# A two-layer graph attention kernel: the order of TensorE's work written out by hand

## The chip, the cores and the metric

The kernel runs on one core of one Trainium2 chip. A core has five engines that run side by side: TensorE (PE, matmuls and transposes; PEld is its weight load), VectorE (DVE), ScalarE (ACT), GpSimd (POOL) and SyncE (SP), which here issues all transfers. Each engine takes its instructions in the order in which the program gives them, and waits at an instruction until what it needs is there. The time is the device time of one execution, in microseconds (us); the figure is the median of three runs.

## The reference, cut to what matters

There are 32 graphs of 512 nodes with 512 features, an adjacency matrix each, and weights that all graphs share. Each graph goes through a normalisation, two attention layers (four heads of 256 features, then one of 512) and a residual sum. All of it is in f32; only the masks are in bf16.

```python
h = relu(layernorm(x))                       # [32, 512, 512]
mask = (adj > 0) | eye(512)
def gat_layer(x, mask, W, a_src, a_dst, bias, concat):
    xl = (x @ W).reshape(B, N, H, F)
    asrc, adst = einsum(xl, a_src), einsum(xl, a_dst)          # [B, N, H]
    e = leaky_relu(asrc[:, :, None] + adst[:, None], 0.2)
    attn = softmax(where(mask, e, -1e9), axis=1)               # over source nodes
    out = einsum('bsdh,bshf->bdhf', attn, xl)
    ...
h = elu(gat_layer(h, mask, W1, att_src1, att_dst1, b1, concat=True))     # 4 heads x 256
out = x + gat_layer(h, mask, W2, att_src2, att_dst2, b2, concat=False)   # 1 head x 512
```

## The kernel before

**Stages of a graph.** A graph's 512 nodes are four tiles of 128 rows. `front` normalises x (VectorE; a power on GpSimd), transposes it on TensorE (`pht`, 16 transposes of 128x128) into `ht`, makes the mask `m` from adj and its transpose `mt` (`pm`, 16 transposes in bf16). `project1`, the first product, makes `xl` in eight accumulator tiles (`pxl`, 16 matmuls each, two heads a tile; two more columns a head hold the scores of the attention vectors, which `weights` folded into W1). `soft` is the softmax of a layer: the scores are transposed to a row (`pas`), stored to DRAM and loaded back spread over all partitions; VectorE takes the masked maximum over each of the 128-row tiles (`junk`, L205: 16 in layer 1, 4 in layer 2); the shifts made from the maxima are transposed (`prr`) and sent the same way; then ScalarE takes two exponentials for each tile of `p` (L227, L230) and VectorE takes their maximum and applies the mask (L234, L235). `gather1` is the first aggregation: for each head two accumulator tiles (`po`, L288, 32 matmuls a head), scaled by the inverse sum into `z`; `turn` transposes `z` (`pz`), and an exponential and two VectorE operations make `h1`, two turns a head. `project2`, the second product, makes `xl2` from `h1` in four tiles of 32 matmuls (`pxm`), each emptied by ScalarE (L315). `gather2` is the second aggregation (`po`, L333, four tiles of 16) and adds x and b2 (`xr`), loaded again and added by GpSimd.

**Order.** The loop of `tile_gat` goes over i. One pass holds the first product of graph i+1, the second aggregation of i-1, the second product of i and the first aggregation of i+1. The other generators (`front` of i+2, the softmaxes) are on a list `side`, and `run` takes one or more of their steps after each step of the main one. This is the order of the program's text; a planner then orders the instructions of each engine by this priority and by its own estimates of when each will be ready. It decides where in TensorE's queue a `prr` or `pas` stands.

**Buffers.** PSUM has eight banks: two accumulator tiles of two banks (tag `mm`), three banks for transposes (`tp`), one for the row turns `pas` and `prr` (`sc`). `xl`, `xl2` and `h1` are there once, `p` four times, the spread rows `orr` twice, `adj` twice, `xr` three times.

Of the kernel before, what the change touches and what calls it, by code (L numbers as in the profile page):

```python
# [28 lines left out]
def tile_gat(  # L29
# [60 lines left out]
    def weights():  # L90
# [30 lines left out]
    def load(b):  # L121
        XT[b], ADJ[b] = [], []
        for t in range(NT):
            xt = work.tile([P, D], F32, tag="x", name=f"x{b}_{t}", bufs=4)
            nc.sync.dma_start(xt, x[b, t * P : (t + 1) * P, :])
            XT[b].append(xt)
            a = work.tile([P, N], I32, tag="adj", name=f"adj{b}_{t}", bufs=2)
# [3 lines left out]
    def front(b):  # L131
# [11 lines left out]
        for t in range(NT):  # L143
# [4 lines left out]
            ps = psum.tile([P, KT, P], F32, tag="tp", name=f"pht{b}_{t}", bufs=3)  # L148
# [4 lines left out]
        del XT[b]  # L153
        m = work.tile([P, NT, N], BF16, tag="m", name=f"m{b}", bufs=3)
# [7 lines left out]
        for d in range(NT):  # L162
            ps = psum.tile([P, N], BF16, tag="tp", name=f"pm{b}_{d}", bufs=3)
# [5 lines left out]
            yield  # L169

    def soft(b, layer, n, cols, give):
# [8 lines left out]
        def spread(v, rows, per, tag, bufs):  # L180
# [4 lines left out]
            sb = work.tile([k, P], F32, tag=f"r{tag}", name=f"r{tag}{name}")  # L185
            nc.vector.tensor_copy(sb, ps)
            dr = dram.tile([k, P], F32, tag=f"d{tag}", name=f"d{tag}{name}")
            nc.sync.dma_start(dr, sb)
            got = []
            for i in range(0, rows, per):  # L190
                o = work.tile([P, per, N], F32, tag=f"o{tag}", name=f"o{tag}{name}_{i}", bufs=bufs)
# [6 lines left out]

        asr = spread(sc[:, 0].rearrange("p h t -> p (h t)"), n, n, "as", 1)[0]
        yield  # L200
        mx = work.tile([P, n, NT], F32, tag=f"mx{layer}", name=f"mx{name}")
        for h in range(n):
            for d in range(NT):
                junk = work.tile([P, N], BF16, tag="junk", name=f"junk{name}_{h}_{d}", bufs=1)
                nc.vector.tensor_tensor_reduce(  # L205
                    out=junk, in0=asr[:, h, :], in1=MASKT[b][:, d, :], scale=1.0, scalar=-BIG,
                    op0=OP.add, op1=OP.max, accum_out=mx[:, h, d : d + 1],
                )
                if d % 2:
                    yield  # L210
        if layer == 2:
            del MASKT[b]
        ad = sc[:, 1]
        top = work.tile([P, n, NT], F32, tag=f"top{layer}", name=f"top{name}")
        nc.vector.tensor_add(top, mx, ad)
        nc.vector.scalar_tensor_tensor(top, top, SLOPE, top, op0=OP.mult, op1=OP.max)
        r = work.tile([P, n, 2, NT], F32, tag=f"r{layer}", name=f"r{name}")
        nc.vector.tensor_sub(r[:, :, 0, :], ad, top)
        nc.vector.scalar_tensor_tensor(r[:, :, 1, :], ad, SLOPE, top, op0=OP.mult, op1=OP.subtract)
        rr = spread(r.rearrange("p h i t -> p (h i t)"), 2 * n, 2, "rr", 2)  # L220
        yield
# [20 lines left out]
    PS1, PS2, H1 = {}, {}, {}  # L242

    def project1(b):
        ht = HT.pop(b)
        for t in range(NT):
            for hp in range(0, H, 2):
                ps = psum.tile([P, 2, 512], F32, tag="mm", name=f"pxl{b}_{t}_{hp}", bufs=2)
                for j in range(2):
                    for k in range(KT):  # L250
                        nc.tensor.matmul(  # L251
                            ps[:, j, :W], ht[:, k, t * P : (t + 1) * P], w1_sb[:, k, hp + j, :],
                            start=(k == 0), stop=(k == KT - 1),
                        )
                nc.scalar.activation(xl[:, t, hp : hp + 2, :W], ps[:, :, :W], AF.Copy)  # L255
                yield
# [4 lines left out]
    def turn(b, h, z):  # L261

        for f in range(FPH):
            g = h * FPH + f
            ps = psum.tile([P, N], F32, tag="tp", name=f"pz{b}_{g}", bufs=3)
# [11 lines left out]
    def gather1(b):  # L277
        H1[b] = work.tile([P, FT, N], F32, tag="h1", name=f"h1{b}", bufs=1)
        turns = []
        for h in range(H):  # L280
            p = PS1.pop((b, h))
            z = work.tile([P, NT, FH], F32, tag="z", name=f"z{b}_{h}")
            for dp in range(0, NT, 2):
                ps = psum.tile([P, 2, 512], F32, tag="mm", name=f"po{b}_{h}_{dp}", bufs=2)
# [17 lines left out]
        yield  # L302

    def project2(b):
        h1 = H1.pop(b)
        for t in range(NT):
            ps = psum.tile([P, 2, 512], F32, tag="mm", name=f"pxm{b}_{t}", bufs=2)
            for k in range(FT):
                for j in range(2):
# [4 lines left out]
                    )  # L314
            nc.scalar.activation(  # L315
                xl2[:, t, : DO + 2].rearrange("p (c w) -> p c w", c=2), ps[:, :, : W - 1], AF.Copy
# [3 lines left out]
    def cols2(sc):  # L320
        nc.vector.tensor_copy(sc[:, 0, 0, :], xl2[:, :, 0])
        nc.vector.tensor_copy(sc[:, 1, 0, :], xl2[:, :, DO + 1])

    def gather2(b):
        p = PS2.pop(b)
        for d in range(NT):
# [38 lines left out]
    def finish():  # L365
        while side:
            for _ in side.pop(0):
                pass
# [58 lines left out]
```

## Time and profile before

| | |
|---|---|
| median of 3 runs | 3809.48 us (3802.36 to 3810.51) |
| the profiled execution: own time / span | 3810.58 / 3808.8 us |
| mean granted TensorE clock | 0.965 |
| busy: PE / PEld / DVE / ACT / POOL | 91% / 77% / 58% / 35% / 6% of the span |
| matmuls and transposes | 16512 |
| transfers | 269.85 MB, 71 GB/s, 21.7% of 16 engines |

The span goes from the first to the last instruction; the execution's own time is a little longer. A matmul's row has a start and a duration that overlaps with the next, so how fast they follow one another is read from starts. An idle time in brackets is that just before the instruction, with what ended it. The granted clock is a share of TensorE's full 2.4 GHz; 0.50 is 1.2 GHz.

### The profile page before, as it was taken

What the parts mean: (1) busy time and instruction counts of PE and PEld (TensorE: products, weight loads), DVE (VectorE), ACT (ScalarE), POOL (GpSimd) and SP (SyncE); (2) the same over time, 40 slices, a digit from 0 to 9 for tenths busy, and PEclk for the clock granted to TensorE, in tenths of its full rate; (3) what the DMA queues carried; (4) which work ended last, traced back from release to release, by engine and by line L of the source; (5) the groups of instructions that cost most, each with busy time, mean ns of one, the idle gap of its engine ahead of it and who ended that gap; (6) DMA issues with size and microseconds to landing.
All of it is one profiled execution on the core that took longest, in us unless ns stands there. A gap on an engine that the chain in (4) does not pass through costs nothing.

```text
span 3808.8 us, 42519 instructions
## 1 busy us (share of the span) xinstructions
PE 3457.8 (91%) x16512; PEld 2950.1 (77%) x16512; DVE 2212.1 (58%) x4549; ACT 1351.1 (35%) x2305; POOL 223.9 (6%) x166
## 2 busy tenths in 40 slices
PE   4889999999999999999999999999999999999997
PEld 3767787877788777788777787777887777887776
DVE  6466556565556565555665555655566655556653
ACT  1343333443323443324433324433234433244331
POOL 0000000000000000000000000000000000000000
PEclk8889999999999999999999999999999999999998
DMA  5112222122222122222122211222221222211111
GB/s 166 39 53 68 78 83 65 55 82 67 79 77 73 53 81 70 78 75 68 60 69 76 84 64 53 81 69 78 76 70 58 79 68 82 75 62 45 64 62 47
DMA packets 115291, 269.85 MB, mean 71 GB/s; under 512 B 14480, under 2 KB 19472, under 8 KB 110992
## 3 DMA queue, kind: packets, MB, share of 16 engines
q1 hardware_dynamic: 115088, 267.12, 21.7%
q8 instruction: 130, 2.13, 0.2%
q14 instruction: 73, 0.60, 0.1%
HBM read 232.53 MB, written 34.54 MB: 70 GB/s over the span
## 4 chain that ended last, share of the span: by engine, by line
PE 63%; DVE 16%; ACT 15%; DMA 4%; issue 2%; SPq 0%; ACTq 0%; POOL 0%; DVEq 0%
PE pxl L251 23%; PE po L288 21%; DVE junk L205 11%; PE po L333 9%; ACT e L230 7%; ACT p L227 7%; PE pxm L310 4%; PE pz L267 3%; DMA orr<-drr 2%; PE pht L150 2%; DVE xr L340 1%; DVE p L235 1%; DMA drr<-rrr 1%; DVE p L234 1%; PE pm L165 1%
## 5 line engine op out<-in xcount | busy, mean ns | idle before, releaser
L288 PE MATMUL po<-xl,p 128*128 128x257 f32 x4096 | 966.0, 391 | 134.2 <-ACT xl L315 109.8
L288 PEld LDWEIGHTS po<-xl,p 128*128 128x128 f32 x4096 | 780.2, 196 | 266.5 <-ACT xl L315 132.8
L310 PE MATMUL pxm<-w_sb,h 128*128 128x257 f32 x4096 | 947.7, 393 | 0.0
L251 PE MATMUL pxl<-w_sb,ht 128*128 128x258 f32 x4096 | 933.4, 382 | 12.6 <-DVE j L101 12.6
L310 PEld LDWEIGHTS pxm<-w_sb,h 128*128 128x128 f32 x4096 | 807.9, 198 | 127.0
L251 PEld LDWEIGHTS pxl<-w_sb,ht 128*128 128x128 f32 x4096 | 761.5, 190 | 115.8 <-DVE j L101 13.6
L234 DVE TENSOR_TENSOR p<-p,e 128x1024 f32<-128x1024 f32 x320 | 391.7, 1224 | 336.9 <-ACT e L230 336.9
L205 DVE CUSTOM_DVE_ANT_0 junk<-oas,mt 128x512 bf16<-128x512 f32 x640 | 542.5, 848 | 44.3 <-DMA oas<-das 27.3
L227 ACT ACTIVATE p<-orr,sc 128x512 f32<-128x512 f32 x640 | 454.7, 711 | 61.4 <-DMA orr<-drr 60.8
L333 PE MATMUL po<-xl,p 128*128 128x256 f32 (+1 forms) x2048 | 456.7, 381 | 10.3 <-DVE p L235 10.3
L230 ACT ACTIVATE e<-orr,sa 128x512 f32<-128x512 f32 x640 | 454.2, 710 | 0.0
L315 ACT ACTIVATE xl<-pxm 128x514 f32<-128x514 f32 x128 | 75.6, 590 | 1036.6 <-PE pxm L310 1036.6
L333 PEld LDWEIGHTS po<-xl,p 128*128 128x128 f32 x2048 | 387.1, 190 | 70.6 <-ACT e L230 10.6
L255 ACT ACTIVATE xl<-pxl 128x516 f32<-128x516 f32 x256 | 153.9, 601 | 691.5 <-PE pxl L251 691.5
L235 DVE TENSOR_TENSOR p<-p,m 128x1024 f32<-128x1024 f32 x320 | 390.7, 1221 | 6.5
L294 ACT ACTIVATE z<-po,inv 128x256 f32<-128x256 f32 x256 | 120.1, 470 | 450.6 <-DVE inv L293 450.6
L329 POOL TENSOR_TENSOR xr<-xr,b_sb 128x512 f32<-128x512 f32 x128 | 190.3, 1490 | 1337.1 <-DMA xr<-in_x_dram 1192.0
L259 DVE COPY sc<-xl 128x32 f32<-128x32 f32 x32 | 6.0, 188 | 404.4 <-ACT xl L255 404.4
L272 ACT ACTIVATE e<-pz,b_sb 128x512 f32<-128x512 f32 x256 | 171.9, 683 | 174.7 <-PE pz L267 165.5
L274 DVE SCALAR_TENSOR_TENSOR h<-pz,b_sb,e 128x512 f32<-128x512 f32 x256 | 190.7, 745 | 6.3
L136 DVE BATCH_NORM_STATS2 stats<-x 128x6 f32<-128x512 f32 x128 | 87.6, 686 | 171.9 <-DMA x<-in_x_dram 171.7
L140 POOL TENSOR_TENSOR rstd<-rstd,half 128x4 f32<-128x4 f32 x32 | 32.9, 1030 | 2239.6 <-DVE rstd L139 2239.6
(48 smaller groups left out, 1395.8 us busy)
## 6 DMA issues: line engine op xcount, KB each, us to landing
orr<-drr SPq DMA_DIRECT2D x160, 512.0 KB
x<-in_x_dram SPq DMA_DIRECT2D x128, 256.0 KB
adj<-in_adj_dram SPq DMA_DIRECT2D x128, 256.0 KB
xr<-in_x_dram SPq DMA_DIRECT2D x128, 256.0 KB
oas<-das SPq DMA_DIRECT2D x32, 1024.0 KB
out_dram<-xr SPq DMA_DIRECT2D x128, 256.0 KB
oas<-das SPq DMA_DIRECT2D x32, 256.0 KB
w_sb<-in_L_gnn_W_dram SPq DMA_DIRECT2D x4, 512.0 KB
```

Of the source, the lines that this page charges most:

```text
L205: nc.vector.tensor_tensor_reduce(out=junk, in0=asr[:, h, :], in1=MASKT[b][:, d, :], scale=1.0, scalar=-BIG, op0=OP.add, op1=OP.max, accum_ ...
L227: nc.scalar.activation(p[:, t + j, :], rr[h][:, 0, :], AF.Exp, bias=sc[:, 0, h, t + j : t + j + 1])
L230: nc.scalar.activation(e2[:, j, :], rr[h][:, 1, :], AF.Exp, bias=sa2[:, h, t + j : t + j + 1])
L234: nc.vector.tensor_max(pp, pp, e2)
L235: nc.vector.tensor_tensor(pp, pp, MASK[b][:, t : t + 2, :], op=OP.min)
L251: nc.tensor.matmul(ps[:, j, :W], ht[:, k, t * P : (t + 1) * P], w1_sb[:, k, hp + j, :], start=(k == 0), stop=(k == KT - 1),)
L272: nc.scalar.activation(e, ps, AF.Exp, bias=bias)
L274: nc.vector.scalar_tensor_tensor(H1[b][:, g, :], ps, bias, e, op0=OP.add, op1=OP.max)
L288: nc.tensor.matmul(ps[:, j, : FH + 1], p[:, s, d * P : (d + 1) * P], xl[:, s, h, 2 : W + 1], start=(s == 0), stop=(s == NT - 1),)
L310: nc.tensor.matmul(ps[:, j, : W - 1], h1[:, k, t * P : (t + 1) * P], w2_sb[:, k, j * (W - 1) : (j + 1) * (W - 1)], start=(k == 0), stop=(k ...
L329: nc.gpsimd.tensor_tensor(xr, xr, b2_sb, op=OP.add)
L333: nc.tensor.matmul(ps[:, j, : hi - lo], p[:, s, d * P : (d + 1) * P], xl2[:, s, lo:hi], start=(s == 0), stop=(s == NT - 1),)
```

## The change

TensorE's order becomes that of the text (`manual_schedule` for PE alone); the planner still orders the other engines. `side`, `run` and `finish` go, and the loop says at which step of which stage each step of another generator stands. The maxima of layer 1 are taken in two groups of two heads, each with its own `prr`, store and loads; the turns stand behind the first and the second tile of the second product. `project2` yields twice a tile. The turns of `z` stand one at a time behind later tiles, the last two in the next graph's first product. `mm` has three tiles, `tp` two, and `pas` and `prr` use `tp`. `front` is split into `norm` and `masks`, whose steps move into the first product and the end of the first aggregation. At the start the first graph's vectors are folded head by head, its first product goes over the first two heads of all tiles first, and the second layer's weights come after the masks. For the last graph `xl2` is laid over `xl`, and its second product stands before the second aggregation of the graph before. Left out below are the renamed parts whose text is the same.

```diff
-    def weights():
+    def weights1():
...
-        for a, v in enumerate((as1, ad1)):
-            for h in range(H):
+        for h in range(H):
+            for a, v in enumerate((as1, ad1)):
...
+    def weights2():
...
-            ps = psum.tile([P, KT, P], F32, tag="tp", name=f"pht{b}_{t}", bufs=3)
+            ps = psum.tile([P, KT, P], F32, tag="tp", name=f"pht{b}_{t}", bufs=2)
...
-            yield
+            if d % 2:
+                yield
...
-            ps = psum.tile([k, P], F32, tag="sc", name=f"p{tag}{name}", bufs=1)
+            ps = psum.tile([k, P], F32, tag="tp", name=f"p{tag}{name}{more}", bufs=2)
...
+        yield
         asr = spread(sc[:, 0].rearrange("p h t -> p (h t)"), n, n, "as", 1)[0]
+        g = min(n, 2)
+        rr = {}
+        for h0 in range(0, n, g):
+            mx = work.tile([P, g, NT], F32, tag=f"mx{layer}", name=f"mx{name}_{h0}")
+            for h in range(h0, h0 + g):
+                for d in range(NT):
...
+            ad = sc[:, 1, h0 : h0 + g]
...
+            yield
+            got = spread(
+                r.rearrange("p h i t -> p (h i t)"), 2 * g, 2, "rr", 2, f"_{h0}"
+            )
+            rr.update({h0 + i: o for i, o in enumerate(got)})
         yield
...
+        steps = [(t, hp) for t in range(NT) for hp in (0, 2)]
+        if b == 0:
+
+            steps = [(t, hp) for hp in (0, 2) for t in range(NT)]
+        for t, hp in steps:
+            ps = psum.tile([P, 2, 512], F32, tag="mm", name=f"pxl{b}_{t}_{hp}", bufs=3)
...
-                if turns:
-                    next(turns[0], None)
                 yield
-            turns = [turn(b, h, z)]
-        for _ in turns[0]:
-            pass
-        yield
+            turns.append(turn(b, h, z))
+
+    def x2(b):
+
+        if b < B - 1:
+            return xl2
+
+        v = bass.AP(
+            tensor=xl.tensor, offset=xl.offset, ap=[xl.ap[0], [DO + 3, NT], [1, DO + 3]]
+        )
+        return v
...
+                if k == FT // 2 - 1:
+                    yield
...
+    def step(g):
+
+        if g is not None:
+            next(g, None)
...
+    def turned():
+        while turns:
+            try:
+                next(turns[0])
+                return
+            except StopIteration:
+                turns.pop(0)
 
     load(0)
-    weights()
...
+    weights1()
+    rest(norm(0))
+    load_adj(0)
+    rest(masks(0))
+    weights2()
+    soft1, soft2 = {}, {}
+    with tc.manual_schedule(engines={mybir.EngineType.PE}):
+        for i in range(-1, B + 1):
+
+            front = i + 2 < B
+            nm = norm(i + 2) if front else None
+            mk = masks(i + 2) if front else None
+            s2 = soft2.get(i - 1)
+            if front:
+                load(i + 2)
+                load_adj(i + 2)
+                step(nm)
+            if i + 1 < B:
+                for n, _ in enumerate(project1(i + 1)):
+                    if n < 2:
+                        turned()
+                    if n < 3:
+                        step(s2)
+                    step(nm)
+                soft1[i + 1] = soft(i + 1, 1, H, cols1, keep1(i + 1))
+            s1 = soft1.get(i + 1)
+            step(s1)
+            rest(s2)
+            last = i == B - 1
+            if last:
+                for _ in range(2):
+                    turned()
+            stages = [gather2(i - 1)] if i >= 1 else []
+            if 0 <= i < B:
+                stages.insert(0 if last else 1, project2(i))
+            n = 0
+            for g in stages:
+                for _ in g:
+                    n += 1
+                    if n in (1, 6, 8):
+                        step(s1)
+                    elif n > 8:
+                        step(s1)
+                        step(s1)
+                    if last and n == 8:
+                        soft2[i] = soft(i, 2, 1, cols2(i), keep2(i))
+                        step(soft2[i])
+                        step(soft2[i])
+                    if last and n == 10:
+                        step(soft2[i])
+            rest(s1)
+            if 0 <= i < B and not last:
+                soft2[i] = soft(i, 2, 1, cols2(i), keep2(i))
+                step(soft2[i])
+            if i + 1 < B:
+                for n, _ in enumerate(gather1(i + 1)):
+                    if n >= 2:
+                        turned()
+                    if n in (1, 4):
+                        step(soft2.get(i))
+                    if n >= 5:
+                        step(mk)
+            elif i < B:
+                rest(soft2[i])
```

## Rows read from the trace of the kernel before

**Rows 1.** Waits of PE, 262.4 to 3725: waiter, releaser, us in total, times, longest.

```profile
PE prr L184 <- DVE r L219: 114.4, 30, 4.4
PE po L288 <- ACT xl L315: 109.8, 49, 4.7
PE pas L184 <- DVE sc L321: 14.8, 11, 1.5
```

**Rows 2.** Timeline, PE: start us, us, engine line op, out<-in, count, [idle before <-releaser].

```profile
1426.48 0.60 PE L150 MATMUL pht<-identf,hn 128*128 128x128 f32 x4
1426.92 3.65 PE L251 MATMUL pxl<-w_sb,ht 128*128 128x258 f32 x16
1430.40 0.61 PE L165 MATMUL pm<-identb,m 128*128 128x128 bf16 x8
1430.85 3.70 PE L251 MATMUL pxl<-w_sb,ht 128*128 128x258 f32 x16
...
1445.11 3.64 PE L333 MATMUL po<-xl,p 128*128 128x256 f32 x16
...
1473.63 0.39 PE L184 MATMUL prr<-identf,r 128*32 128x128 f32 x1 [4.33 <-DVE r L219]
1473.82 20.25 PE L310 MATMUL pxm<-w_sb,h 128*128 128x257 f32 x82
1496.03 3.73 PE L288 MATMUL po<-xl,p 128*128 128x257 f32 x16 [1.95 <-ACT xl L315]
```

**Rows 3.** Windows: stretch, length, busy (count) by engine, granted clock, DMA share, GB/s.

```profile
1473.60:1478.00 4.40, 4.37 (x11) 3.54 (x12) 0.28 (x1) 0.00 (x0) 0.00 (x0) 0.50 0.28 68
1496.00:1501.40 5.40, 3.73 (x16) 2.96 (x16) 4.80 (x6) 5.40 (x10) 0.00 (x0) 1.00 0.00 0
```

**Rows 4.** Timeline, PE: first products of graphs 1 and 2, last first aggregation.

```profile
144.70 0.60 PE L251 MATMUL pxl<-w_sb,ht 128*128 128x258 f32 x2
...
260.11 0.60 PE L251 MATMUL pxl<-w_sb,ht 128*128 128x258 f32 x2
...
3719.60 3.63 PE L288 MATMUL po<-xl,p 128*128 128x257 f32 x16
```

**Rows 5.** Timeline, DVE and POOL, row maxima of one graph, 1456 to 1474.

```profile
1456.73 0.68 DVE L205 CUSTOM_DVE_ANT_0 junk<-oas,mt 128x512 bf16<-128x512 f32 x1
1457.09 1.45 POOL L329 TENSOR_TENSOR xr<-xr,b_sb 128x512 f32<-128x512 f32 x1 [28.80 <-DMA xr<-in_x_dram]
...
1457.45 1.64 DVE L205 CUSTOM_DVE_ANT_0 junk<-oas,mt 128x512 bf16<-128x512 f32 x1
...
1464.28 1.63 DVE L205 CUSTOM_DVE_ANT_0 junk<-oas,mt 128x512 bf16<-128x512 f32 x1
...
1473.41 0.17 DVE L219 SCALAR_TENSOR_TENSOR r<-sc,top 128x16 f32<-128x16 f32 x1
```

**Rows 6.** Timeline, ACT, before the first aggregation of the same graph.

```profile
1500.16 0.71 ACT L230 ACTIVATE e<-orr,sa 128x512 f32<-128x512 f32 x1
1500.78 0.58 ACT L315 ACTIVATE xl<-pxm 128x514 f32<-128x514 f32 x1
```

**Rows 7.** Groups, L272: line engine op, shapes, count | busy, mean ns | idle.

```profile
L272 ACT ACTIVATE e<-pz,b_sb 128x512 f32<-128x512 f32 x256 | 171.9, 683 | 174.7 <-PE pz L267 165.5 <-DVE h L274 9.0
```

**Rows 8.** Timeline, PE, start of the program, 54 to 102.

```profile
54.08 1.13 PE L150 MATMUL pht<-identf,hn 128*128 128x128 f32 x8 [3.75 <-DVE hn L145]
...
71.39 0.28 PE L184 MATMUL pas<-identf,sc 128*16 128x128 f32 x1 [0.91 <-DVE sc L259]
...
101.53 8.85 PE L288 MATMUL po<-xl,p 128*128 128x257 f32 x29 [10.76 <-DVE p L235]
```

**Rows 9.** Timeline, PE, end of the program, 3768 to 3788.

```profile
3768.45 0.27 PE L184 MATMUL pas<-identf,sc 128*4 128x128 f32 x1 [0.89 <-DVE sc L321]
3777.18 0.37 PE L184 MATMUL prr<-identf,r 128*8 128x128 f32 x1 [8.46 <-DVE r L219]
3787.85 16.51 PE L333 MATMUL po<-xl,p 128*128 128x256 f32 x64 [10.29 <-DVE p L235]
```

More of the change, by code (lines that the diff above doesn't have):

```diff
@@ L126, in load, with load_adj @@
             XT[b].append(xt)
+    def load_adj(b):
+        for t in range(NT):
             a = work.tile([P, N], I32, tag="adj", name=f"adj{b}_{t}", bufs=2)
@@ L153, in front, with masks @@
         del XT[b]
+    def masks(b):
         m = work.tile([P, NT, N], BF16, tag="m", name=f"m{b}", bufs=3)
@@ L162, in front @@
         for d in range(NT):
-            ps = psum.tile([P, N], BF16, tag="tp", name=f"pm{b}_{d}", bufs=3)
+            ps = psum.tile([P, N], BF16, tag="tp", name=f"pm{b}_{d}", bufs=2)
             for t in range(NT):
@@ L178, in soft, with spread @@
         q = n * NT
-        def spread(v, rows, per, tag, bufs):
+        def spread(v, rows, per, tag, bufs, more=""):
             k = rows * NT
-            ps = psum.tile([k, P], F32, tag="sc", name=f"p{tag}{name}", bufs=1)
+            ps = psum.tile([k, P], F32, tag="tp", name=f"p{tag}{name}{more}", bufs=2)
             nc.tensor.transpose(ps, v, identf)
-            sb = work.tile([k, P], F32, tag=f"r{tag}", name=f"r{tag}{name}")
+            sb = work.tile([k, P], F32, tag=f"r{tag}", name=f"r{tag}{name}{more}")
             nc.vector.tensor_copy(sb, ps)
-            dr = dram.tile([k, P], F32, tag=f"d{tag}", name=f"d{tag}{name}")
+            dr = dram.tile([k, P], F32, tag=f"d{tag}", name=f"d{tag}{name}{more}")
             nc.sync.dma_start(dr, sb)
@@ L190, in spread @@
             for i in range(0, rows, per):
-                o = work.tile([P, per, N], F32, tag=f"o{tag}", name=f"o{tag}{name}_{i}", bufs=bufs)
+                o = work.tile([P, per, N], F32, tag=f"o{tag}", name=f"o{tag}{name}{more}_{i}", bufs=bufs)
                 nc.sync.dma_start(
@@ L242, in tile_gat @@
     PS1, PS2, H1 = {}, {}, {}
+    turns = []
     def project1(b):
         ht = HT.pop(b)
[L246 to L256, printed above, removed]
+        steps = [(t, hp) for t in range(NT) for hp in (0, 2)]
[3 more added lines that the diff above has]
+            ps = psum.tile([P, 2, 512], F32, tag="mm", name=f"pxl{b}_{t}_{hp}", bufs=3)
+            for j in range(2):
+                for k in range(KT):
+                    nc.tensor.matmul(
+                        ps[:, j, :W], ht[:, k, t * P : (t + 1) * P], w1_sb[:, k, hp + j, :],
+                        start=(k == 0), stop=(k == KT - 1),
+                    )
+            nc.scalar.activation(xl[:, t, hp : hp + 2, :W], ps[:, :, :W], AF.Copy)
+            yield
     def cols1(sc):
@@ L264, in turn @@
             g = h * FPH + f
-            ps = psum.tile([P, N], F32, tag="tp", name=f"pz{b}_{g}", bufs=3)
+            ps = psum.tile([P, N], F32, tag="tp", name=f"pz{b}_{g}", bufs=2)
             for d in range(NT):
@@ L283, in gather1 @@
             for dp in range(0, NT, 2):
-                ps = psum.tile([P, 2, 512], F32, tag="mm", name=f"po{b}_{h}_{dp}", bufs=2)
+                ps = psum.tile([P, 2, 512], F32, tag="mm", name=f"po{b}_{h}_{dp}", bufs=3)
                 for j in range(2):
@@ L329, in gather2 @@
             nc.gpsimd.tensor_tensor(xr, xr, b2_sb, op=OP.add)
-            ps = psum.tile([P, 2, 512], F32, tag="mm", name=f"po2{b}_{d}", bufs=2)
+            ps = psum.tile([P, 2, 512], F32, tag="mm", name=f"po2{b}_{d}", bufs=3)
             for s in range(NT):
@@ L350, in keep2 @@
         return lambda h, p: PS2.__setitem__(b, p)
-    side = []
-    def run(main, per):
-        for _ in main:
-            for _ in range(per):
-                while side:
-                    try:
-                        next(side[0])
-                        break
-                    except StopIteration:
-                        side.pop(0)
[L365 to L368, printed above, removed]
-    load(0)
-    weights()
-    for _ in front(0):
-        pass
@@ new lines, in rest @@
+    def rest(g):
+        for _ in g or ():
+            pass
+    def turned():
[5 more added lines that the diff above has]
+                turns.pop(0)
+    load(0)
+    weights1()
[61 more added lines that the diff above has]
+                rest(soft2[i])
```

77 lines of the change are left out of this document (27 added, 50 removed).

## The prediction

> **What bounds the kernel now.** I read the page first: TensorE's matmuls are busy 91% of the span, VectorE 58%, ScalarE 35%, the transfers 22%. So the time is TensorE's work plus the idle time between. The list of who TensorE waited for comes next. The reader is to see in it that, over the 30 full graphs, almost all waiting has two causes, each about once or twice a graph: a row turn (`prr`) that waits for the row maxima on VectorE, and the first aggregation matmuls (`po`) that wait for ScalarE to empty an accumulator of the second product [rows 1]. Then the order of time inside one graph: TensorE takes instructions in order, so at 1473.63 one small transpose holds back 82 matmuls that were ready [rows 2]; the table of stretches shows that the wait is paid twice, since after it the granted clock is 0.50 (1.2 GHz) for 4.4 us, about 2.2 us of lost work, while in the stretch behind the 1.95 us wait at 1496.03 it stays 1.00 (2.4 GHz) [rows 3]. The start and the end of the program are read by themselves, further down.
>
> **TensorE's own work in a graph.** 16 matmuls take 3.48 us from start to start (1426.92 to 1430.40), so 0.2175 each; four f32 transposes 0.44; eight bf16 ones 0.45 [rows 2]. A graph has 128 matmuls in the first product, 128 in the second, 128 in the first aggregation, 64 in the second: 448 x 0.2175 = 97.4. It has 48 f32 transposes (5.3), 16 bf16 ones (0.9) and, after the change, five row turns at about 0.1 (0.5; now four). Sum 104.1. The 30 graphs from 260.11 to the end of the last first aggregation, 3719.60 + 16 x 0.2175 = 3723.1, take 3463.0, or 115.4 each [rows 4]. So 11.3 us a graph are not work: the listed waits are 241 us, 8.0 a graph [rows 1], the low clock 2.2 [rows 3], the rest starts after waits.
>
> **The change, part by part, in one of these 30 graphs.** Times are counted from the end of the first product (1445.11 in the trace).
>
> *The row turns.* The first half's `prr` is now written behind the second aggregation (64 x 0.2175 = 13.9), one `pas` (0.1) and the first tile of the second product (6.96): at 20.9. It needs half of the 16 row maxima. The eighth begins at 1464.28 and takes 1.63, and four small operations end at 0.73 behind the last maximum, as now in the step that ends with L219 [rows 5]: 1464.28 + 1.68 + 0.73 - 1445.11 = 21.6. TensorE waits 0.7. The other half is written 6.96 later, at 28.7 with that wait. Now all 16 are turned at 1473.63, 28.5 [rows 2]; the four small operations twice and a copy of `prr` between put it at 29.5, another 0.8. So about 1.4 in place of 3.8 (114.4 over 30 [rows 1]). Bounds: 0, if the maxima begin as soon as their row lands, and 4.4, the wait now. Both waits stay under the 1.95 that left the clock alone, so the 2.2 of low clock go too. Behind a waiting turn stand all of the second product's matmuls.
>
> A maximum takes 0.68 alone and 1.64 when GpSimd's addition of `xr` overlaps it; three of the first eight were held so, about 0.95 each [rows 5]. The Trainium skill, SBUF — State Buffer, section "SBUF: two separate sides", says that a VectorE operation with two SBUF inputs and a GpSimd one exclude each other for a whole instruction. By that rule one addition may cost its full 1.45, and three of them would put the first turn 1.5 us later, 45 us over 30 graphs; the trace's 0.95 agrees with a block whose first part was over.
>
> *Three accumulators.* `po` waited 109.8 over 30 graphs, 3.7 each, because it needs the slot of the tile before last; ScalarE empties the last tile only at 1500.78, behind softmax exponentials [rows 1, 6]. With three slots the first `po` takes the slot of the second tile, done 14 us earlier, and the next the third tile's, 7 us earlier; the row shows the last tile emptied 6.7 us after its end (1496.03 - 1.95 = 1494.08 [rows 2]). That just fits. I take 0 left; bounds 0 and 3.7.
>
> *Two transposition slots instead of three, shared with the row turns.* Most are written one at a time, a 3.48 us block apart. In the last two blocks of the first aggregation there are three in a row: one of `z`, two of masks. The third needs a slot: that of the mask before it, free after VectorE's copy. No row shows it with two slots. Nearest from below 0 (VectorE at once, as nearly now: no such wait in [rows 1]); from above a `z` turn's own release, through an exponential of 0.68 [rows 7] and two VectorE operations, about 2.3 (an estimate: three times 0.68 and the starts). I take 1.0 twice, nearest the copy: 2.0, bounds 0 to 4.6.
>
> *The rest.* The second layer's `pas` waits 0.5 (14.8 over 30 [rows 1]) as now, its `prr` perhaps 0.2. Steps of masks, norm and softmax that are moved issue the same instructions; on VectorE, ScalarE and the transfer queue the planner still chooses the order. The sixteen exponential pairs' work (some 20 us each on ScalarE and VectorE) starts some 7 us earlier, since the first half of the rows is sent 20.9 and not 28.5 after the mark, so `p` of the first head is there before 42.5, where the first aggregation starts. The second turn adds to each graph one copy, one store and four small operations: about 1 us of VectorE's 69 busy in 116, beside TensorE's work but for the waits counted above, and one issue on SyncE. The load of the third head's rows still holds SyncE's queue until the first head's exponentials free a buffer, with the stores of `out` and the next loads behind it, as now; there it costs nothing as long as `xr` is a graph ahead. If the lead of `p` were gone, `po` would wait instead of `prr`.
>
> Sum: 104.1 + 1.4 + 0 + 2.0 + 0.7 = 108.2 for 115.4. Times 30, less about 4.6 for the last (no norm, masks or their waits): 3241 for 3463, **-222**. (The 115.4 average has that lack in it.)
>
> **Start.** Now the first product ends at 71.39 - 0.91 = 70.5, the first `po` is at 101.53, and graph 1's first product begins at 144.70 [rows 4, 8]. After: by-head order lets the first four tiles start with half the vectors, but each tile is followed by a transpose of graph 1's norm, which came only at 54.08 [rows 8], behind weights' work on VectorE. If norm fits into VectorE's gaps between the vectors, at about 39 (an estimate), the product ends at 67; if it stays at 54, seven tiles of 3.48 and 1.7 put it at 80. I take 67.6 (-2.9), bounds 60 and 81. To the first `po`: 31.0 now, less eight maxima at 0.73, 25.2 (-5.8). The first aggregation: 43.2 now; 30.4 of work, 2.4 low clock, 3.0 for `z` behind `p` on VectorE, 2.5 masks: 38.3 (-4.9). Together **-13.6**.
>
> **Graph 1** has no second aggregation: 115.4 now [rows 4]. After: 104.1 - 13.9 = 90.2; the first half's turn at 20.9 plus 10.7 from a `prr` to the first use of its `p` (3777.18 to 3787.85 [rows 9]) against 28.1 gives a wait of 3.5 with 2.2 low clock; `z` behind `p` 4; masks 2 and 0.5: 102.4, **-13.0**.
>
> **End.** From 3723.1 to 3808.8: 85.7. The second product of the last graph now comes before the previous graph's aggregation, so that its softmax has 13.9 us of cover. Now the waits are 0.89, 8.46 and 10.29 [rows 9]. After: 0.9; 8.7 - 7.0 = 1.7; 10.7 - 7.0 = 3.7. Gain 13.3, and 2.6 of low clock in the last 64 matmuls (16.5 for 13.9); against that, the last two turns of `z` stand there without cover, 2.0: **-14**.
>
> Span: 3808.8 - 222 - 13.6 - 13.0 - 14 = 3546. The profiled execution's own time is 1.8 above its span, and the median of the three runs 1.1 below that: 3547.
>
> **Rivals.** (A) A wait returns at a written turn: the first half late by what all 16 are now, 4.4 with 2.2 of low clock instead of 1.4: +5.2 x 30, **3703**. For it: the slack is negative already. Against: only half the maxima are needed. (B) No short wait matters: 104.6 a graph, -3.6 x 30, **3439**. For it: the trace has few waits for masks now. (C) The third accumulator doesn't do what it says, as ScalarE lags by another block: +3.7 x 30, **3658**. For it: 6.7 of 7 us are used. (D) Slower than before: an exponential of a `z` turn stands behind up to eight softmax exponentials (4.9 us at 0.62 [rows 6]) on ScalarE, and holds one of only two slots, with all of TensorE behind it; before there were three and a separate one for rows. Eight turns a graph x 1.5 us more would be 12 a graph: **3907**. It decides from (3808 - 3546) / 30 = 8.7 us a graph. Against: softmax is ahead by 7 us. (E) Short waits lower the clock: five a graph, each with 2.2 as behind the 4.33 one: +11 x 30, **3877**. The trace speaks against it at 1.95 [rows 3]. The Trainium skill, TensorE: Matmul & The Clock Gate, section "A second HAM failure mode: psum-queue depth-cycling", tells of frequent short idle times that make the clock swing; by it this rival would hold, and no run shows it here.
>
> **How the numbers follow.** Forecast 0.72 (own range 3485 to 3620: the bounds of slots 2.6, turns 3.0, start 14). A 0.08, B 0.07, C 0.05, D 0.05, E 0.03. The range leaves out D, E and most of A: 3450 to 3685. About 0.2% is what can be told from no change; faster is the forecast, B, C and most of A, 0.90; same 0.02 from A's upper end; slower 0.08 (D, E).
>
> **What would show it.** Right: `prr` waits per graph near 1.4 with no stretch at 0.50, no wait of `po` for L315's successor, graphs 108 us apart, the first half's exponentials some 7 us earlier, a wait under 4 us before the last 64 matmuls. Wrong: masks or `z` turns waiting more than 5 us a graph, graphs above 113, a first product that ends after 75, or a granted clock below 1 in the 30 graphs.

## The result, and the profile after

The changed kernel takes 3692.8 us (median of 4 runs, 3692.5 to 3693.4), the ratio to before is 0.970, interval 0.9683 to 0.9716. The forecast was 3547 in a range of 3450 to 3685: right in direction, less than half of the gain. The profiled span is 3691.1, TensorE's mean granted clock 0.976.

Set against the forecast's own parts: graph 1's first product begins at 146.8 (forecast 131.1), graph 1 takes 108.6 (102.4), the next 29 graphs 112.1 each (108.2; before 115.6), and the stretch from the last graph's first product to the end 185.5 (175.3). The 29 graphs make up 112 of the 145 us that were missed, the start 16, the end 10, graph 1 6.

The waits of PE over 30 graphs, 255.4 to 3611, to set beside [rows 1] (waiter, releaser, us in total, times, longest):

```profile
PE pm L173 <- DVE mt L176: 69.5, 58, 2.7
PE pz L287 <- ACT z L313: 37.5, 27, 1.4
PE prr L193 <- DVE r L227: 32.8, 30, 2.7
PE pz L287 <- DVE z L314: 17.9, 51, 1.0
```

The two causes of before are gone or smaller: `po` no longer waits for ScalarE (109.8 before), `prr` waits 33 us and not 114. Two new ones stand in their place: the masks' transposes (`pm`), 2.3 us a graph, which the forecast had at 2.0, and the turns of `z` (`pz`), 1.85 a graph, which it had at nothing. In all the waits are 5.3 a graph, where 4.1 was forecast. That is a third of the 3.9 that were missed in a graph. TensorE's timeline of one graph, to set beside [rows 2], shows more. The graph is not a typical one: its wait for a row turn is the longest of the 30, which are 1.1 on average.

```profile
1405.45 3.64 PE L366 MATMUL po<-xl,p 128*128 128x256 f32 x16
...
1429.28 0.38 PE L193 MATMUL prr<-identf,r 128*16 128x128 f32 x1 [2.68 <-DVE r L227]
1429.45 8.69 PE L337 MATMUL pxm<-w_sb,h 128*128 128x257 f32 x32
1437.98 0.27 PE L193 MATMUL prr<-identf,r 128*16 128x128 f32 x1
...
1478.69 0.39 PE L173 MATMUL pm<-identb,m 128*128 128x128 bf16 x4
1479.59 0.38 PE L173 MATMUL pm<-identb,m 128*128 128x128 bf16 x4 [0.51 <-DVE mt L176]
...
1483.77 0.39 PE L173 MATMUL pm<-identb,m 128*128 128x128 bf16 x4
1485.94 0.38 PE L173 MATMUL pm<-identb,m 128*128 128x128 bf16 x4 [1.78 <-DVE mt L176]
```

Counted from the end of the first product (1405.45, the mark below), the first row turn is at 23.8, after a wait of 2.68; forecast were 21.6 and 0.7. The 32 matmuls behind it take 1437.98 - 1429.45 = 8.5 us and not 7.0: the clock is low here too (0.50; columns as in [rows 3]).

```profile
1429.30:1432.60 3.30, 3.30 (x9) 2.65 (x10) 3.20 (x10) 0.00 (x0) 0.00 (x0) 0.50 0.00 0
```

A pair of mask transposes stands behind each of two turns of `z`; the second of each pair waits 0.51 and 1.78. A wait costs about 0.17 more than its row says. It is counted from the end of the row before, and the last instruction of that row would have overlapped with the next one: four transposes that follow one another at 0.055 have a row of 0.39. So 1483.77 + 4 x 0.055 + 1.78 = 1485.77, and the start is 1485.94.

VectorE and ScalarE in the same graph:

```profile
1424.09 1.63 DVE L217 CUSTOM_DVE_ANT_0 jk<-oas,mt 128x512 bf16<-128x512 f32 x1
...
1431.95 0.27 DVE L195 COPY rrr<-prr 16x128 f32<-16x128 f32 x1
...
1437.59 0.72 ACT L243 ACTIVATE p<-orr,sc 128x512 f32<-128x512 f32 x1 [10.35 <-DMA orr<-drr]
...
1460.32 1.22 DVE L251 TENSOR_TENSOR p<-p,m 128x1024 f32<-128x1024 f32 x1
```

A maximum held by GpSimd takes 1.63 as before [rows 5]. The copy of the turned row (L195) begins at 1431.95, 2.7 us after the turn, because VectorE takes four maxima of the second half first. So the first exponential comes at 32.1 after the mark. In the kernel before it came at 1480.69 - 1445.11 = 35.6, and the forecast had it some 7 us earlier, at about 28.6:

```profile
1480.69 0.71 ACT L227 ACTIVATE p<-orr,sc 128x512 f32<-128x512 f32 x1
```

VectorE is full with `p` to 1461.5, 56 us after the mark, and the first turn of `z` starts at 57. In this graph it just fits. In most it doesn't (`pz` waits 27 times for ScalarE's scaling in the 30 graphs), as at 1012 (timeline of all engines, four graphs earlier):

```profile
1012.72 1.21 DVE L251 TENSOR_TENSOR p<-p,m 128x1024 f32<-128x1024 f32 x1
...
1012.86 0.33 PE L287 MATMUL pz<-identf,z 128*128 128x128 f32 x1 [0.45 <-DVE z L314]
1013.86 0.16 DVE L312 RECIPROCAL inv<-po 128x2 f32<-128x2 f32 x1
...
1014.05 0.47 ACT L313 ACTIVATE z<-po,inv 128x256 f32<-128x256 f32 x1 [2.54 <-DVE inv L312]
...
1014.58 0.33 PE L287 MATMUL pz<-identf,z 128*128 128x128 f32 x1 [1.39 <-ACT z L313]
...
1015.10 0.33 PE L287 MATMUL pz<-identf,z 128*128 128x128 f32 x1 [0.19 <-DVE z L314]
```

The last `p` operation runs to 1013.9, only then come the reciprocal of `z`'s second tile and ScalarE's scaling, and the third transpose starts after them. The stretches before and behind this place:

```profile
1000.00:1011.00 11.00, 11.00 (x53) 9.55 (x52) 10.18 (x13) 11.00 (x19) 0.00 (x0) 1.00 0.14 49
1016.30:1019.60 3.30, 3.30 (x9) 2.56 (x9) 1.81 (x4) 0.00 (x0) 0.00 (x0) 0.50 0.21 79
```

The clock is 1.00 (2.4 GHz) before, and 0.50 (1.2 GHz) behind three waits of 0.45, 1.39 and 0.19 us that lie close together. By the trace's granted clock the 30 graphs have 24 such falls to 0.50: 21 behind stops at turns of `z`, three behind a row turn. They cost 43 us, 1.4 a graph; in the kernel before it was 82 us, 2.7 a graph.

Start and end (PE timeline):

```profile
50.75 1.08 PE L155 MATMUL pht<-identf,hn 128*128 128x128 f32 x4 [21.43 <-DVE hn L150]
...
79.38 0.28 PE L193 MATMUL pas<-identf,sc 128*16 128x128 f32 x1 [0.91 <-DVE sc L279]
```

The first transposes of graph 1's norm, which before waited to 54.08 with the first product more than half done [rows 8], now hold that product for 21.4 us; it ends at 78.5 and not 70.5.

```profile
3614.98 1.11 PE L287 MATMUL pz<-identf,z 128*128 128x128 f32 x4 [1.80 <-DVE h L294]
3615.89 30.31 PE L337 MATMUL pxm<-w_sb,h 128*128 128x257 f32 x128
...
3656.38 0.27 PE L193 MATMUL prr<-identf,r 128*8 128x128 f32 x1 [2.06 <-DVE r L227]
...
3670.02 16.70 PE L366 MATMUL po<-xl,p 128*128 128x256 f32 x64 [6.40 <-DVE p L251]
```

At the end the turns of `z` wait 3.0 us in all, and low clock follows twice: 128 matmuls take 30.3 and not 27.8, the last 64 16.7 and not 13.9. The waits before the last 64 are 2.06 and 6.40 where before they were 8.46 and 10.29 [rows 9].

### The profile page after: what moved, and what is told of

The parts are those of the page before. It is cut to its first block, busy times and chain, and to the rows that moved or that the text cites. A ratio compares the mean times of both kernels' runs of the same rounds, so it can differ in the third digit from the quotient of the medians.

```text
span 3691.1 us, 42808 instructions
## 1 busy us (share of the span) xinstructions
PE 3432.2 (93%) x16544; PEld 2948.3 (80%) x16544; DVE 2228.1 (60%) x4710; ACT 1338.1 (36%) x2305; POOL 220.8 (6%) x166
## 4 chain that ended last, share of the span: by engine, by line
PE 52%; DVE 23%; ACT 15%; DMA 7%; issue 3%; SPq 0%; ACTq 0%; POOL 0%; DVEq 0%
PE pxl L271 24%; PE po L307 12%; DVE jk L217 9%; PE po L366 9%; ACT e L246 7%; ACT p L243 6%; DVE p L250 4%; DMA orr<-drr 4%; DVE p L251 3%; PE pxm L337 3%; PE pz L287 2%; DMA drr<-rrr 2%; PE pht L155 1%; DVE xr L373 1%; DVE z L314 1%
## 5 line engine op out<-in xcount | busy, mean ns | idle before, releaser
L271 PE MATMUL pxl<-w_sb,ht 128*128 128x258 f32 x4096 | 921.7, 382 | 7.4 <-DVE j L101 7.4
L337 PE MATMUL pxm<-w_sb,h 128*128 128x257 f32 x4096 | 911.6, 382 | 0.0
L307 PEld LDWEIGHTS po<-xl,p 128*128 128x128 f32 x4096 | 795.0, 198 | 129.5 <-ACT e L246 13.6
L337 PEld LDWEIGHTS pxm<-w_sb,h 128*128 128x128 f32 x4096 | 776.3, 191 | 117.6
L217 DVE CUSTOM_DVE_ANT_0 jk<-oas,mt 128x512 bf16<-128x512 f32 x640 | 538.1, 841 | 55.3 <-DMA oas<-das 45.0
L366 PEld LDWEIGHTS po<-xl,p 128*128 128x128 f32 x2048 | 387.2, 190 | 67.0 <-issue 7.1
L287 PE MATMUL pz<-identf,z 128*128 128x128 f32 x1024 | 175.4, 280 | 66.4 <-ACT z L313 40.2
L287 PEld LDWEIGHTS pz<-identf,z 128*128 128x128 f32 x1024 | 130.4, 142 | 113.1 <-ACT z L313 47.1
```

What stands on the lines that cost most here:

```text
L217: nc.vector.tensor_tensor_reduce(out=junk, in0=asr[:, h, :], in1=MASKT[b][:, d, :], scale=1.0, scalar=-BIG, op0=OP.add, op1=OP.max, accum_ ...
L271: nc.tensor.matmul(ps[:, j, :W], ht[:, k, t * P : (t + 1) * P], w1_sb[:, k, hp + j, :], start=(k == 0), stop=(k == KT - 1),)
L287: nc.tensor.transpose(ps[:, d * P : (d + 1) * P], z[:, d, f * P : (f + 1) * P], identf)
L307: nc.tensor.matmul(ps[:, j, : FH + 1], p[:, s, d * P : (d + 1) * P], xl[:, s, h, 2 : W + 1], start=(s == 0), stop=(s == NT - 1),)
L337: nc.tensor.matmul(ps[:, j, : W - 1], h1[:, k, t * P : (t + 1) * P], w2_sb[:, k, j * (W - 1) : (j + 1) * (W - 1)], start=(k == 0), stop=(k ...
L366: nc.tensor.matmul(ps[:, j, : hi - lo], p[:, s, d * P : (d + 1) * P], v[:, s, lo:hi], start=(s == 0), stop=(s == NT - 1),)
```

## The experiments

The kernels ran in four groups, each group on one chip together with the kernel before; ratios are to that, with the 95% interval. The changed kernel has 0.970. 0.001 is 3.8 us.

Two theories were set against each other. Theory 1: the losses are local; each wait belongs to a place that the written order puts too early, and goes when that place is moved. Theory 2: they are one chain; VectorE's work from the first row turn to the scaling of `z` ends too late, whatever the place, so a wait that is moved comes back further on.

**Four places, one at a time.** `turn_later`: each turn of `z` one block later.

```diff
-                    if n < 2:
+                    if n < 3:
                         turned()
...
-                for _ in range(2):
+                for _ in range(3):
                     turned()
...
-                    if n >= 2:
+                    if n >= 3:
                         turned()
```

> Theory 1 (the turns of z are written one block too early: they wait for z, which stands behind the softmax on VectorE, and the low clock follows that wait): with each turn one block later the waits of pz on z (55.5 us over 30 graphs, about 86 waits with 0.17 of start each) and the low clock behind them (about 1.6 us a graph) go: 3.9 us a graph, 117 us in all, about 3575. Theory 2 (VectorE supplies too slowly as a whole, and the wait moves to the next place, an accumulator or a mask): no more than a third of that, 3650 or above.

0.9732 (0.9715 to 0.9749): no gain. Its waits, 255.4 to 3400:

```profile
PE prr L193 <- DVE r L227: 93.3, 56, 2.6
...
PE po L307 <- DVE z L314: 14.8, 23, 0.9
```

`pz` waits for `z` no more, but `prr` waits 93 us in place of 31 in this stretch (56 times and not 28): TensorE comes to the second layer's row turn (`128*8`, 61 of the 93 us) sooner, and its maxima aren't done. Theory 1 falls for this place: the wait moved on.

`prr_later`: both row turns of layer 1 half a tile later.

```diff
-                    if n in (1, 6, 8):
+                    if n in (1, 7, 9):
                         step(s1)
-                    elif n > 8:
+                    elif n > 9:
```

> Both row turns half a tile (3.48 us) later. Theory 1 (each wait is local): the 33 us of prr waits with their starts go, about 1.3 us a graph, 3655. Theory 2 (the row turns feed the softmax, and what they lose comes back in z): the exponentials start 1.5 to 2.5 us later, pz waits grow by as much and take low clock with them, 3690 to 3740.

0.9874 (0.9852 to 0.9896), 3758.5 us, about 66 us slower than the change and beyond what either theory had:

```profile
PE pz L287 <- ACT z L313: 58.7, 27, 3.3
PE pz L287 <- DVE z L314: 56.6, 54, 1.1
```

The waits of `prr` are gone, and those of `pz` grow from 52 to 115 us in the same stretch, with more low clock (mean of the program 0.966 for 0.976). The first row turn sets when the softmax runs, and what it loses comes back with interest in `z`. That is theory 2, at a higher price than it gave.

`pm_apart`: the mask transposes one each behind the last four tiles of the next first product.

```diff
             nc.vector.tensor_scalar_add(MASKT[b][:, d, :], ps, -BIG)
-            if d % 2:
-                yield
+            yield
...
             mk = masks(i + 2) if front else None
+            mks[i + 2] = mk
...
                     step(nm)
+                    if n >= 4:
+                        step(mks.get(i + 1))
...
-                    if n >= 5:
+                    if n == 5:
                         step(mk)
```

> The four mask transposes of a graph go one each behind the last four tiles of the next first product, in place of two pairs behind turns of z. Theory 1 (they wait because two slots are shared with a turn that stands just ahead): the 69.5 us of pm waits over 30 graphs and their starts (2 x 0.17 a graph) go, 2.6 us a graph, 3612. Theory 2 (VectorE is late for the masks wherever they stand): pm waits stay above 1 us a graph, 3650 or above.

0.9494 (0.9475 to 0.9513), 3610.9 us; a graph 109.4 for 112.1. Theory 1 holds for this place: the waits of `pm` are gone from the 30 graphs, and little took their place (`pht`, 6.6 us).

`w2_later`: the second layer's weights are folded after the first graph's first product.

```diff
     rest(masks(0))
-    weights2()
...
                     step(nm)
+                if i < 0:
+                    weights2()
                 soft1[i + 1] = soft(i + 1, 1, H, cols1, keep1(i + 1))
```

> The second layer's weights are folded after the first graph's first product instead of before it. Theory 1 (the 21.4 us wait for hn at the start comes from the weights' work ahead of it on VectorE): the wait falls to under 5 us, and the program to about 3670. Rival (graph 1's x comes late from memory, or the folding then delays the first maxima): the gain is under 6 us, 3685 or above.

0.9663 (0.9646 to 0.9681), 3677.0 us, 14 us less by the ratios: the wait for graph 1's `hn` falls from 21.43 to 3.00 us, and graph 1 starts at 135.7 and not 146.8. Theory 1 holds for this place too. Some of the gain goes again where the next row turn, `pas`, waits 5.25 us for VectorE and not 0.91.

```profile
31.49 1.09 PE L155 MATMUL pht<-identf,hn 128*128 128x128 f32 x4 [3.00 <-DVE hn L150]
```

**What makes the softmax late, and what the parts are worth.** `no_b2` leaves GpSimd's addition out, so b2 isn't added at all.

```diff
             nc.sync.dma_start(xr, x[b, d * P : (d + 1) * P, :])
-            nc.gpsimd.tensor_tensor(xr, xr, b2_sb, op=OP.add)
```

> The change as it is, without the addition of b2 on GpSimd (the output lacks b2). Theory 2, in its present form (the softmax of layer 1 is fed late, because the maxima before the first row turn are held up by GpSimd's additions, and all later stops follow from its end on VectorE): the first row turn is ready 2.9 us earlier, the waits of prr go (33 us), pz waits fall by half or more, and the low clock behind both: 2.5 to 4.5 us a graph, 3560 to 3620. Theory 1 (each wait local): only the prr waits go, 1.3 us a graph, about 3655.

0.9379 (0.9365 to 0.9393), 3572.2 us: 122 us less than the change, as theory 2 had it. Its waits and its stretch, 255.4 to 3400:

```profile
PE pm L173 <- DVE mt L176: 70.6, 59, 2.8
PE prr L193 <- DVE inv L312: 6.0, 20, 0.8
PE pz L287 <- DVE z L314: 5.3, 28, 0.2
PE pz L287 <- ACT z L313: 2.8, 4, 1.1
```

```profile
255.40:3400.00 3144.60, 3059.26 (x15051) 2648.31 (x15051) 1900.93 (x4172) 1212.81 (x2093) 28.21 (x28) 1.00 0.23 75
```

The wait of `prr` for `r` is gone, `pz` waits 8 us and not 52, and the clock is 1.00 and not 0.99. So 4 us a graph hang on four maxima that GpSimd holds up, one for each of its additions, three of them ahead of the first row turn (in the whole trace of the change 117 of 640 maxima take over 1 us, and 98 us more than the others do): one delay at the head of the chain, paid at the row turn, at `z`, and in the clock. Of the 41 us that low clock costs the change in this stretch, 3 are left here. The Trainium skill, SBUF — State Buffer, section "SBUF: two separate sides", has a VectorE operation with two SBUF inputs and a GpSimd one exclude each other for a whole instruction; here a held maximum takes 1.63 for 0.69, which agrees. The prediction's 45 us by that rule are not this price: they were what the rule would have added to the hold that the rows showed, and at the first row turn alone.

`two_acc`: banks as before the change.

```diff
-            ps = psum.tile([P, 2, 512], F32, tag="mm", name=f"pxl{b}_{t}_{hp}", bufs=3)
+            ps = psum.tile([P, 2, 512], F32, tag="mm", name=f"pxl{b}_{t}_{hp}", bufs=2)
...
-            ps = psum.tile([P, KT, P], F32, tag="tp", name=f"pht{b}_{t}", bufs=2)
+            ps = psum.tile([P, KT, P], F32, tag="tp", name=f"pht{b}_{t}", bufs=3)
...
-            ps = psum.tile([k, P], F32, tag="tp", name=f"p{tag}{name}{more}", bufs=2)
+            ps = psum.tile([k, P], F32, tag="sc", name=f"p{tag}{name}{more}", bufs=1)
```

> The change with the banks as before it: two accumulator tiles, three for transposes, one for row turns. If the third accumulator matters as the prediction had it, po waits for ScalarE's last tiles again, up to 3.7 us a graph, while the 2.6 us of the masks' waits go: 3690 to 3730. If the earlier softmax alone had freed ScalarE, po doesn't wait and the masks' waits go: about 3615.

0.9573 (0.9558 to 0.9587), 3645.5 us: 48 us faster than the change, between the two expectations.

```profile
PE po L307 <- DVE z L314: 72.6, 28, 2.7
PE prr L193 <- DVE r L227: 33.6, 28, 2.4
PE po L307 <- ACT xl L344: 29.8, 25, 2.2
```

`pm` and `pz` wait no more, and `po` waits instead, less for ScalarE (29.8) than for `z` (72.6). Inside this change, the bank given to the third accumulator is taken from masks that need it more.

`one_turn`: one row turn for four heads.

```diff
-        g = min(n, 2)
+        g = n
...
-                    if n in (1, 6, 8):
+                    if n in (1, 8):
```

> The change with one row turn for all four heads, behind the second tile of the second product. Theory 2: the exponentials start about 6 us later than with halves, p reaches the first head just as the first aggregation begins and z comes 4 to 6 us later, with low clock: 3800 to 3880, so the halves carry more than the whole gain. If only the place of the turn matters, one wait of about 0.5 us: 3670 to 3700.

0.9909 (0.9894 to 0.9924), 3773.9 us: 80 us slower than the change. The direction is that of theory 2, the size between the two: `prr` hardly waits, but `pz` does (73 us) and the second layer's `pas` (55).

`combo1`: `pm_apart`, `w2_later`, `turn_later`, and

```diff
-                    if n in (1, 4):
+                    if n in (1, 5):
                         step(soft2.get(i))
```

> pm_apart, w2_later and turn_later together, and the second layer's row turn one block later too. If the waits of turn_later only moved to that row turn because it stayed in place: pm 2.6, z 3.9 a graph and 16 at the start off, about 3480. If VectorE has no room after the softmax whatever the places: as pm_apart and w2_later alone, 3590.

0.9286 (0.9268 to 0.9303), 3538.3 us, midway between the two: with its next stop moved as well, the later turns of `z` do pay, but not all that they waited.

**The written order by itself.** `planner`: the changed text, TensorE's order left to the planner.

```diff
-    with tc.manual_schedule(engines={mybir.EngineType.PE}):
+    if True:
```

> The change's text with TensorE's order left to the planner again. If the written order is what pays, the planner puts row turns and turns of z by its own estimates, without GpSimd's hold on the maxima, and the time goes back to 3750 to 3810. If the text's halves and slots pay and the order alone is worth little, 3640 to 3720.

0.9421 (0.9407 to 0.9436), 3589.0 us: 106 us faster than the same text with the order written down, and outside both expectations. A graph takes 109.5, graph 1 starts at 127.8. The row turns and turns of `z` stand at the same places and wait no less (41 and 57 us from 255.4 to 3400, for 31 and 52); the difference is in the masks (PE timeline):

```profile
1106.62 0.39 PE L173 MATMUL pm<-identb,m 128*128 128x128 bf16 x4
1106.85 1.09 PE L307 MATMUL po<-xl,p 128*128 128x257 f32 x4
1107.77 0.39 PE L173 MATMUL pm<-identb,m 128*128 128x128 bf16 x4
```

The planner takes the second mask transpose four matmuls later, and `pm` waits 0.4 us in place of 66 in the same stretch. At the start it lets matmuls pass the norm of graph 1. The graphs make 2.6 x 30 = 78 of the 106 us, the start 19; so most of the price of the written order lies at these two places, as `pm_apart` (2.7 a graph) and `w2_later` (14) had shown from the other side.

`before_no_b2`: the kernel before, likewise without b2.

```diff
-            nc.gpsimd.tensor_tensor(xr, xr, b2_sb, op=OP.add)
```

> The kernel before without the addition of b2 on GpSimd (the output lacks b2). If the wait of 4.33 us for the row turn is the hold of GpSimd's additions on about five maxima (5 x 0.95 = 4.7 us), that wait and its 2.2 us of low clock go and po waits for ScalarE less: 6 to 8 us a graph, 3570 to 3630. If the maxima are late for another reason (their row lands late), under 2 us a graph, 3750 or above.

0.9754 (0.974 to 0.9769), 3715.2 us: 93 us less, 3.1 a graph, and neither of the two. Waits, 255.4 to 3400:

```profile
PE po L288 <- ACT xl L315: 116.5, 33, 5.5
PE pas L184 <- DVE sc L321: 30.6, 23, 1.5
PE prr L184 <- DVE r L219: 11.9, 28, 0.4
```

The wait that was 4.33 us goes (the longest is 0.4), which settles its cause, though the hold is on four maxima a graph here too and not on the five of the expectation. Of its 114 us and the low clock behind it, some 66 by the 2.2 of one graph [rows 1, 3], half comes back: TensorE arrives sooner, and `po` and `pas` wait longer for tiles that ScalarE empties behind its exponentials (`po` 99 and `pas` 15 us in the same stretch of the kernel before).

`combo2`: `combo1`, with b2 added where VectorE empties the second product (b2 gets a column of zeros on either side, for the two score columns).

```diff
-            nc.scalar.activation(
-                v[:, t, : DO + 2].rearrange("p (c w) -> p c w", c=2), ps[:, :, : W - 1], AF.Copy
-            )
+            nc.vector.tensor_tensor(
+                v[:, t, : DO + 2].rearrange("p (c w) -> p c w", c=2), ps[:, :, : W - 1],
+                b2_sb.rearrange("p (c w) -> p c w", c=2), op=OP.add,
+            )
...
-            nc.gpsimd.tensor_tensor(xr, xr, b2_sb, op=OP.add)
```

> combo1, and b2 is added where VectorE empties the second product's tiles (in place of ScalarE's copy), since the weights of a row sum to one; GpSimd's additions go, and the output is whole. If GpSimd's hold is what still makes the row turns wait (55.9 us of prr, 25.5 of po on z in combo1): 1.5 to 2.5 us a graph less, 3460 to 3495. If VectorE's four more operations a graph (0.75 each, among p) give it back: 3530 to 3550.

0.9061 (0.9046 to 0.9076), 3451.4 us: better than expected. Waits and stretch, 255.4 to 3400:

```profile
PE pht L156 <- DVE h L294: 6.4, 7, 2.2
PE pz L287 <- DVE h L294: 6.3, 2, 4.0
...
```

```profile
255.40:3400.00 3144.60, 3131.10 (x15468) 2717.90 (x15467) 2001.40 (x4391) 1186.31 (x2026) 28.38 (x27) 1.00 0.24 77
```

Some 13 us of waits are left in 30 graphs, the clock is 1.00, and a graph takes 104.7 on average, most of them 104.3 to 104.6. That is nearly the forecast's 104.1 of work: TensorE has almost nothing left to wait for.

`combo2_planner` (the edit of `planner` on `combo2`) and `combo2_two_acc` (that of `two_acc`):

> combo2 with TensorE's order left to the planner. If the written order cost time in the change only through two badly chosen places (masks in pairs, the norm of graph 1 ahead of its x), then with these mended the planner can gain nothing: 3445 to 3470, the same within 0.5%. If the planner's order is better or worse in itself, 3400 or 3500.

> combo2 with two accumulator tiles, three slots for transposes and one for row turns. If the third accumulator is worth what the prediction took it for (po waits 3.7 us a graph without it): 3550 to 3570. If an earlier softmax has made it needless: within 10 us of 3451.

0.9015 (0.8994 to 0.9036), 3433.8 us, and 0.9317 (0.9298 to 0.9335), 3547.8 us. The planner still wins a little, a bit more than the first expectation had; by the traces 2 us of it lie before graph 1, 7 in the graphs between and 7 from the start of the last graph's first product on. It is the fastest kernel here. Two accumulators cost 96 us there, 3.2 a graph, with one wait for it:

```profile
PE po L307 <- DVE z L314: 65.3, 29, 2.5
```

So the third accumulator is worth about what the forecast had (3.7), but by another way: here it covers `z`. ScalarE's copies, which the forecast named, are not in this kernel, where VectorE empties those tiles; where they are, in `two_acc`, they take 30 us of `po`'s waits and `z` takes 73.

Not tried: the kernel before with three accumulators alone, and its old text with TensorE's order written down.

## Why the prediction was wrong

**TensorE's work, right.** 104.1 a graph was forecast; `combo2` shows 104.3 in most graphs.

**The row turns, right in kind, and too small in effect.** 1.4 was forecast for the waits, 1.1 measured; that the sums are near is in part luck, since it is one turn that waits, and the second's 0.8 didn't come. But "so `p` of the first head is there before 42.5" and rival D's "softmax is ahead by 7 us" looked at `po` only. The step left out what VectorE does after `p`: the scaling of `z`, which the written order needs at 54. And it left out that the turned row's copy waits in VectorE's queue behind the other half's maxima. Rival D had the turns of `z` as the place of the loss, but by ScalarE's queue; the trace has VectorE's.

**The turns of `z`, the step that failed.** "Most are written one at a time, a 3.48 us block apart" gave them no wait. They wait 1.85 a graph. The forecast had seen `z` behind `p` on VectorE, and counted 3.0 for it at the start and 4 in graph 1, but nothing in the 30 graphs. `prr_later` and `no_b2` show the cause: the end of `p` on VectorE, which follows from the first row turn, which follows from GpSimd's hold on the maxima. `turn_later` shows that the place alone doesn't cure it.

**The clock, the other failed step.** "Both waits stay under the 1.95 that left the clock alone, so the 2.2 of low clock go too." It drew a bound from one wait [rows 3]. After, the clock falls behind a wait of 1.39 us with 0.45 just before it and 0.19 just behind, and three times behind a single one of 1.94 to 2.68 (last section). In a graph 112.1 - 104.1 - 5.3 = 2.7 us are neither work nor listed wait. 168 waits in 30 graphs cost 0.17 each beyond their rows, 0.95 a graph; the forecast had seen such time in the kernel before ("the rest starts after waits") and put none in its sum. Some 1.7 is left for low clock, of which the trace's granted clock shows 1.4. So about half of the low clock of before went, and not all. Rival E was half right, at a sixth of its price. The Trainium skill, TensorE: Matmul & The Clock Gate, section "A second HAM failure mode: psum-queue depth-cycling", tells of frequent short idle times that make the clock swing; the trace after agrees, with 0.50 behind three waits of under 1.4.

**The masks, right.** 2.0 forecast, 2.3 measured, and `pm_apart` and `two_acc` (three slots) show the two shared slots as the cause.

**The third accumulator, right in size by luck** (3.7 forecast, 3.2 in `combo2_two_acc`), wrong in way; in the change itself, with the masks' slots as its price, it loses 48 us (`two_acc`).

**The start, inside its bounds** (60 to 81 for the end of the first product, 78.5 measured), at the end I had not chosen: the norm did wait for the weights' work, as `w2_later` and `planner` show. Graph 1 missed by 6 us: its mean clock is 0.94, some 7 us of low clock where 2.2 was forecast, and `po` waits 5.4 for `p` where 3.5 was; `z`, at 3.7, waits as forecast (4). The end missed by 10: the last wait is 6.40 and not 3.7, `z` waits 3.0 and not 2.0, and the low clock in two stretches of matmuls costs 2.5 and 2.8 where none was forecast.

**What the forecast never asked** is what the written order does by itself. `planner` shows it as a loss of 106 us; the gain is that of the other parts, of which the halves are worth 80 (`one_turn`). With the two bad places mended the loss is 18 us (`combo2` against `combo2_planner`).

**The forecast's own signs of being wrong.** Two of its four came: a first product that ends after 75 (78.5), and a granted clock below 1 in the 30 graphs. On average graphs stayed under 113 (112.1), and neither masks nor `z` waited more than 5 a graph.

## What to carry to other kernels

When one engine's order is written by hand, follow the chain of the other engines past the first consumer: the wait that is taken away comes back where the same slow engine is next needed, and each short wait there also costs start time and clock. Before moving a place, look for what delays the head of the chain; here a small addition on another engine was worth more than any one place (122 us in `no_b2`, 78 in `pm_apart`). And try the new text with the old scheduler, since parts that are made together need not pay together.

## What was not expected of the hardware

The granted clock falls behind waits much shorter than the 4.33 us of the kernel before: to 0.50 after 0.45, 1.39 and 0.19 us close together, and to 0.50 after a single wait of 1.94 us in the trace after, while 1.95 us in the kernel before left it at 1.00 [rows 3]. So the length of the wait alone doesn't decide, and what else does stays open.

```profile
2886.02 0.28 PE L193 MATMUL prr<-identf,r 128*16 128x128 f32 x1 [1.94 <-DVE r L227]
...
2886.80:2890.10 3.30, 3.30 (x9) 2.60 (x8) 3.20 (x10) 0.00 (x0) 0.00 (x0) 0.50 0.01 3
```

Each wait of TensorE costs about 0.17 us beyond what its row lists: the overlap of one instruction with the next, which the wait takes away.
